# Attention and a gated feed-forward on one core: where transposes and projections stand among the score tiles

## The chip, the core and the metric

The kernel runs on one core of a Trainium2 chip. The metric is the time of one execution on the device in microseconds (us), as the median of several runs. A core has five engines that work side by side and wait for each other through semaphores: TensorE (PE in the profile; its loading of weights is the row PEld), VectorE (DVE), ScalarE (ACT), GpSimd (POOL) and SyncE (SP), which here only starts transfers. Every engine takes its instructions in the order of the program.

## The reference, cut to what matters

Sixteen heads of width 8 over 32 sequences of 256 tokens with 128 features; the distance of two tokens is subtracted from their score. Then a feed-forward of four layers in two halves, and a normalisation after each part.

```python
scores = jnp.einsum('bhid,bhjd->bhij', Q, K) / jnp.sqrt(jnp.float32(hd))
scores = jnp.where(causal_mask, -jnp.inf, scores) + decay
attn = jax.nn.softmax(scores, axis=-1)
out = jnp.einsum('bhij,bhjd->bhid', attn, V) ... @ Wo.T + bo
x = _layernorm(x + out)
h = jax.nn.silu(_tlin(x, w1_w, w1_s)) * _tlin(x, w2_w, w2_s)
h = jax.nn.gelu(_tlin(h, h1_w, h1_s), approximate=False)
h = jax.nn.gelu(_tlin(h, h2_w, h2_s), approximate=False)
x = _layernorm(x + _tlin(h, w3_w, w3_s))
```

## The kernel before

Two sequences make a pair, and there are 16 pairs. `step(n)` (L725) works on several pairs at once: it finishes the attention of pair n, finds the row maxima of pair n+1, projects the queries and keys of pair n+2, ends the feed-forward of pair n-2 and does that of pair n-1. Its first half is a loop of 12 turns (L733), numbered i = 0 to 11 here; its second half is the feed-forward `feed(n - 1)` (L793) with what is left of the attention (`rest`, L761) between its products. The steps from n = 2 to n = 13 are alike; n = 0, 1, 14 and 15 lack some parts.

What a turn of the loop holds, for these steps:

- `weigh(n, i)` (L430): one tile of transposed scores on PE, which the profile calls `s<-qs,ks`, then the exponential on ACT (`e`) and the causal selection on POOL. Every third tile (i = 2, 5, 8, 11) takes the blocks that stand wholly on the diagonal and is called `s_0d` to `s_3d`.
- `row_maxima(n+1, i)` (L373): the same scores the other way round, `s<-ks,qs`, four small products that add the mask (`s<-tri_q,ident_b`), and a maximum on DVE (`m<-s`).
- in some turns a filler on PE. `project(n+2)` (L314, the generator `ahead`) has three: four transposes of x (`pxT`, copied by DVE as `xT`), the queries (`pq`, read by ACT as `qhi` and by DVE as `qlo`) and the keys (`pk`). `last(n-2)` (L648, the generator `settling`) has two: the last layer (`pw3` in the code, shown as `pw<-heven`, which ACT turns into `yT`) and four transposes (`py`, which DVE adds to x1 as `y`). `turn(n-1)` (L538) transposes x1 (`px1T`). `outputs(n, a)` (L470, the generator `side`) has the head outputs `pa` of three score tiles, in two portions, and for every second a the copy `oT` on ACT, four transposes `pt` and the division on DVE (`rec`, `on`).
- at i = 3 DVE also writes the four pieces of `z` for the pair before (`late`, L738).

Two pools in PSUM bind the engines to each other. All score tiles share three buffers of two banks (`ps_s`, L283, tag `s`): a tile can be filled when the one three places earlier has been read, which for `s<-ks,qs` is the exponential of the turn before, and for `s<-qs,ks` the maximum of two turns before. All else shares two buffers of one bank (`ps_w`, L284, tag `work`): `pa` keeps one of them from i = 3 to the copy `oT` at i = 7, and in that time `py`, `pq` and `pk` follow each other through the other one.

The order of all this is written out by hand in the loop, and nothing reorders it (`InOrder`, L50).

PE's products use its array in four ways, which the profile's rows show as rows*columns of the weights: the whole array (128*128: transposes, projections, feed-forward), two halves by rows (64*128 or 62*128: scores), quarters (64*64: the mask), and four strips of columns (128*32: head outputs).

Of the kernel before, what the change touches and what calls it, by code (L numbers as in the profile page):

```python
# [33 lines left out]
G, C = 4, 4  # L34
# [27 lines left out]
def tile_attn_ffn(  # L62
# [96 lines left out]
    def prepare(func):  # L159

        act.activation(nothing, half[:, 0:1], func)
# [124 lines left out]
    def work(nm):  # L286
        return ps_w.tile([P, 512], F32, name=nm, tag="work")

    def two(nm):
        return ps_s.tile([P, 2, 512], F32, name=nm, tag="s")  # L290
# [82 lines left out]
    def row_maxima(n, i):  # L373

        q, k, m = (pairs[n][w] for w in "qkm")
        mv = m.rearrange("i b c (e p g) -> i e p g b c", e=2, p=2)[:, i // 6]
        a, part = divmod(i, 3)
        if part < 2:
            g = 2 * a + part
            s = two(f"s1_{n}_{g}").rearrange("i p (b j) -> i p b j", b=2)  # L380
            for b in range(2):
                for p in range(2):
                    rows = slice(64 * p, 64 * p + ROWS1)
                    pe.matmul(
                        s[:, p, b, :], lhsT=q[rows, g, b * T + P : (b + 1) * T],
                        rhs=k[rows, g, b * T : (b + 1) * T], start=(b == 0), stop=False,
                    )
            mask(lambda p: (s[:, p], P, 2))
            vec.tensor_reduce(mv[:, :, g % C, :, 1], s, AX.X, ALU.max, negate=True)
            return  # L390
        s = two(f"s1_{n}_{a}d").rearrange("i p (h b j) -> i p h b j", h=2, b=2)
        for h in range(2):
            for b in range(2):
                for p in range(2):
                    rows = slice(64 * p, 64 * p + ROWS1)
                    i0 = b * T
                    pe.matmul(
                        s[:, p, h, b, :], lhsT=q[rows, 2 * a + h, i0 : i0 + P],
                        rhs=k[rows, 2 * a + h, i0 : i0 + P],
                        start=(h == 0 and b == 0), stop=False,  # L400
                    )
        mask(lambda p: (s[:, p].rearrange("i h b j -> i (h b) j"), 0, 4))
        vec.tensor_reduce(
            mv[:, :, 2 * a % C : 2 * a % C + 2, :, 0], s, AX.X, ALU.max, negate=True
        )

    def maxima_to_rows(n, halves=(0, 1)):

        q, m = pairs[n]["q"], pairs[n]["m"]
        pm = work(f"pm_{n}_{halves[0]}")  # L410
        e0, rows = halves[0], W * len(halves)
        for t in range(NT):
            pe.transpose(
                pm[0:rows, t * P : (t + 1) * P],
                m[:, t // 2, t % 2, W * e0 : W * e0 + rows], ident,
            )
        hi = mp.tile([H, TOK], F32R, name=f"mhi_{n}_{e0}", tag="mhi", bufs=1)
        act.copy(hi[0:rows, :], pm[0:rows, :])
        lo = mp.tile([H, TOK], F32R, name=f"mlo_{n}_{e0}", tag="mlo", bufs=1)
        vec.tensor_tensor(  # L420
            lo[0:rows, :], pm[0:rows, :], hi[0:rows, :].bitcast(F32), ALU.subtract
        )
        for i, e in enumerate(halves):
            for r, part in enumerate((hi, lo)):
                sp.dma_start(
                    out=q[ROWS1 + r :: 64, C * e : C * e + C, :].bitcast(F32),
                    in_=part[W * i : W * i + W, :].bitcast(F32),
                )
# [41 lines left out]
    def outputs(n, a):  # L470
        v = pairs[n]["v"]
        *first, second = pairs[n][("e", a)]
        r, e = divmod(a, 2)
        if e == 0:
            pairs[n]["pa"] = work(f"pa_{n}_{r}").rearrange("c (b i) -> c b i", b=2)
        pa = pairs[n]["pa"]
        for jc in range(2):
            for b in range(2):
                for c in range(C):
                    h, p = c // 2, c % 2  # L480
                    at = VSLOT * (C * r + c) + VHEAD * e
                    pe.matmul(
                        pa[32 * c : 32 * (c + 1), b, jc * P :],
                        lhsT=v[:, 2 * b + jc, at : at + 32],
                        rhs=second[:, p, h, b, :] if jc else first[h][:, p, b, :],
                        start=(e == b == jc == 0), stop=(e == b == jc == 1),
                        tile_position=(0, 32 * c),
                    )
            if jc == 0:
                yield  # L490
        if e == 0:
            return
        oT = op.tile([P, TOK], F32, name=f"oT_{n}_{r}", tag="oT", bufs=1)
        act.copy(oT, pa.rearrange("c b i -> c (b i)"))
        yield

        if r == 0:
            pairs[n]["on"] = op.tile([P, NT, D], F32, name=f"on_{n}", tag="on", bufs=1)
        on = pairs[n]["on"].rearrange("i t (r e c d) -> i t r e c d", r=2, e=2, c=C)
        po = work(f"pt_{n}_{r}").rearrange("i (t c k) -> i t c k", t=NT, c=C)  # L500
        for t in range(NT):
            pe.transpose(po[:, t].rearrange("i c k -> i (c k)"), oT[:, t * P : (t + 1) * P], ident)
        yield
        rec = mp.tile([P, NT, C, 2], F32, name=f"rec_{n}_{r}", tag="rec")
        vec.reciprocal(rec, po[:, :, :, HD : HD + VHEAD + 1 : VHEAD])
        for e in range(2):
            vec.tensor_tensor(
                on[:, :, r, e], po[:, :, :, VHEAD * e : VHEAD * e + HD],
                rec[:, :, :, e : e + 1].to_broadcast([P, NT, C, HD]), ALU.mult,
            )  # L510
# [19 lines left out]
    def first_norm(n):  # L530
        x1 = x1s[n % 3]
        yield from layernorm(pairs[n]["xb"], x1, f"a_{n}")
        pairs[n] = dict(x1=x1)
# [145 lines left out]
    def run(gen):  # L679
        for _ in gen:  # L680
            pass


    ahead = project(0)
# [7 lines left out]
    ahead = project(1)  # L692
# [32 lines left out]
    def step(n, exact=None, ws=None, hp=None, gp=None):  # L725


        side = iter(())
        settling = (
            last(n - 2, exact, ws, gp) if n > 1 else first_norm(0) if n else inexact_weights()  # L730
        )
        ahead = project(n + 2) if n + 2 < NPAIR else iter(())
        for i in range(3 * G):  # L733
            weigh(n, i)
            j = i + {0: LEAD, 1: -LAG}.get(n, 0)
            if n + 1 < NPAIR and 0 <= j < 3 * G:
                row_maxima(n + 1, j)
            if i == 3 and late:  # L738
                run(late.pop())
            next(side, None)  # L740
            if n and i == 9:
                turn(n - 1, exact)
            if i in ((0, 2) if n > 1 else (0, 2, 4, 6)) if n else i < 11:
                next(settling, None)

            if i in ((3, 4, 5) if n == 1 else (1, 3, 5)):
                next(ahead, None)
            if i % 3 == 2:
                run(side)
                side = outputs(n, i // 3)  # L750
            if n == 0 and i == 3 * G - LEAD:
                maxima_to_rows(1)
        if n < 2:
            run(settling)
        run(ahead)
        if n + 2 < NPAIR:
            stack(n + 2, "q")
            stack(n + 2, "k", sp if n else act)


        def rest():  # L761
            for _ in range(3):
                next(side)
                yield
            if n == 1:
                for i in range(3 * G - LAG, 3 * G):
                    row_maxima(2, i)
                    yield
            if 0 < n < NPAIR - 1:
                maxima_to_rows(n + 1)  # L770
            run(side)
            yield
            if n + 2 < NPAIR:
                project_values(n + 2)
                yield
            last_steps = finish(n)
            next(last_steps)
            yield
            yield from last_steps
            if n:  # L780
                yield
                yield from first_norm(n)
            if n == NPAIR - 1:
                yield
                turn(n, exact)
            if n > 1:
                next(settling)
                late.append(settling)

        if n:  # L790
            prepare(AF.Silu)
        due = rest()
        for _ in feed(n - 1, exact, ws, hp, gp) if n else ():  # L793
            next(due, None)
        run(due)
# [85 lines left out]
```

## Time and profile before

| | us |
|---|---|
| median of 3 runs | 823.32 (823.05 to 824.74) |
| the profiled execution | 824.06 |
| its span, first to last instruction | 822.2 |
| PE busy | 784.6 (95%) |
| DVE busy | 636.0 (77%) |
| ACT busy | 527.5 (64%) |
| POOL busy | 260.8 (32%) |

In the span's 12 alike steps a loop of 12 turns takes 23.27 us (318.45 to 341.72 of the span, the step n = 6), with PE busy for all of it, DVE for 19.90 us and ACT for 16.48 us; the second half of that step takes 24.1 us more. The granted clock of PE is 1.00 there.

How to read the rows: a row of the timeline gives the start in the span, the length, the engine, the line, the operation, out<-in, the shape and how many in a row are merged. Matmuls overlap each other, so the length of a row is longer than the time until the next one starts; what a group of products costs PE is the distance from its start to the start of the next group. In brackets stands the idle time ahead of an instruction and who ended it.

### The profile page before, as it was taken

Reading aid. Unit: us, or ns where it says so; the run is one execution under the profiler, and the core shown is the slowest. Engines: PE = TensorE matmul, PEld = TensorE weight load, DVE = VectorE, ACT = ScalarE, POOL = GpSimd, SP = SyncE. Lnnn points to the kernel's source line nnn. Section 1 sums busy time; section 2 is a strip of 40 time slices with the busy share of each in tenths; the row PEclk is TensorE's granted clock in tenths of the full one; section 3 lists DMA queues with packets and bytes.
Section 4 is the critical chain, followed back from the end, with each engine's and each line's share of the span. In section 5 each row is a group of like instructions: output and inputs, shape, how many; then the busy total and the mean of one; then the engine's idle time right before and its main releaser. Section 6 shows DMA issues by size and latency. Waiting matters only on the chain.

```text
span 822.2 us, 17431 instructions
## 1 busy us (share of the span) xinstructions
PE 784.6 (95%) x7046; PEld 555.8 (68%) x7046; DVE 636.0 (77%) x1247; ACT 527.5 (64%) x719; POOL 260.8 (32%) x341
## 2 busy tenths in 40 slices
PE   4896999999999999999999999999999999999994
PEld 2664676776767677676767767676767767666673
DVE  6786778877887887778788877888878787873674
ACT  5065556766666766766576676667666666758572
POOL 5033413333142333414232342424243231424211
PEclk9879999999999999999999999999999999999998
DMA  6824140403204140410404040130404022000001
GB/s 147 213 62 106 29 92 14 106 15 74 60 14 106 28 107 14 92 42 21 110 17 106 27 101 20 43 90 15 107 26 104 4 62 59 14 4 14 1 8 37
DMA packets 39898, 47.49 MB, mean 58 GB/s; under 512 B 3968, under 2 KB 21632, under 8 KB 39808
## 3 DMA queue, kind: packets, MB, share of 16 engines
q1 hardware_dynamic: 37152, 42.82, 22.0%
q10 hardware_dynamic: 2656, 3.48, 1.9%
q8 instruction: 57, 0.93, 0.5%
q14 instruction: 33, 0.27, 0.1%
HBM read 7.48 MB, written 4.19 MB: 14 GB/s over the span
## 4 chain that ended last, share of the span: by engine, by line
PE 83%; DVE 4%; ACT 3%; issue 1%; DMA 0%; POOL 0%; ACTq 0%; POOLq 0%; DVEq 0%
PE peven L58 14%; PE podd L58 14%; PE s L58 12%; PE pa L58 11%; PE pw L58 10%; PE s_2d L58 2%; PE s_3d L58 2%; PE po L58 2%; PE s_0d L58 2%; PE s_1d L58 2%; PE pt L58 2%; PE pv L58 2%; PE pk L58 2%; PE pq L58 2%; PE px1T L58 1%; PE py L58 1%
## 5 line engine op out<-in xcount | busy, mean ns | idle before, releaser
L58 DVE TENSOR_REDUCE m<-s 128x4 f32<-128x1024 f32 x128 | 155.5, 1218 | 14.6 <-PE s L58 13.3
L58 ACT ACTIVATE e<-s 128x1024 f32<-128x1024 f32 x128 | 130.7, 1022 | 44.2 <-PE s L58 34.2
L463 POOL TENSOR_SCALAR_AFFINE_SELECT e<-e 128x512 f32<-128x512 f32 x128 | 82.6, 646 | 218.5 <-ACT e L58 189.3
L58 PE MATMUL podd<-h,h_near 128*128 128x512 f32 x512 | 131.3, 403 | 1.0 <-DVE m L58 0.5
L58 PE MATMUL peven<-hodd,h_near 128*128 128x512 f32 x512 | 122.7, 396 | 0.0
L58 PEld LDWEIGHTS peven<-hodd,h_near 128*128 128x128 f32 x512 | 95.7, 187 | 23.4 <-DVE hodd L58 0.3
L58 PEld LDWEIGHTS podd<-h,h_near 128*128 128x128 f32 x512 | 91.8, 188 | 23.1 <-DVE h L58 3.2
L58 ACT ACTIVATE hodd<-podd,sh 128x512 fp32r<-128x512 f32 x64 | 44.0, 688 | 62.7 <-PE podd L58 62.6
L58 PE MATMUL pw<-x1T,w_near 128*128 128x512 f32 x256 | 75.6, 418 | 1.1 <-DVE h0w L58 1.1
L274 POOL TENSOR_TENSOR rsa<-rsa,half 128x4 f32<-128x4 f32 x16 | 16.3, 1018 | 176.7 <-DVE rsa L58 176.7
L58 DVE SCALAR_TENSOR_TENSOR h0w<-pw,s,sg 128x512 f32<-128x512 f32 x64 | 47.9, 748 | 30.4 <-ACT sg L58 30.4
L58 PEld LDWEIGHTS s<-qs,ks 64*128 64x128 f32 x512 | 38.9, 188 | 47.7 <-issue 34.1
L58 PE MATMUL pa<-e,vaug 128*32 128x256 f32 x1024 | 70.6, 389 | 0.0
L58 PE MATMUL s<-qs,ks 64*128 64x256 f32 x512 | 65.3, 335 | 0.6 <-ACT e L58 0.5
L58 DVE TENSOR_TENSOR heven<-evenw,heven 128x512 fp32r<-128x512 f32 x64 | 44.2, 692 | 26.6 <-ACT evenw L58 26.1
L58 ACT ACT_TABLE_LOAD x47 | 60.3, 1283 | 3.4 <-issue 2.6
L58 ACT ACTIVATE sg<-pw,s 128x512 f32<-128x512 f32 x64 | 43.7, 684 | 28.2 <-PE pw L58 27.9
L58 PE MATMUL s<-ks,qs 62*128 62x256 f32 x512 | 56.9, 302 | 2.4 <-ACT e_0d L58 1.8
L58 ACT ACTIVATE heven<-peven,sh 128x512 fp32r<-128x512 f32 x48 | 33.4, 696 | 39.8 <-PE peven L58 39.8
L58 PEld LDWEIGHTS pw<-x1T,w_near 128*128 128x128 f32 x256 | 43.4, 188 | 18.4 <-ACT nothing L58 5.8
L581 POOL TENSOR_TENSOR h<-h0w,h 128x512 fp32r<-128x512 f32 x31 | 40.0, 1291 | 43.5 <-DVE h L58 41.2
L58 DVE TENSOR_TENSOR hodd<-oddw,hodd 128x512 fp32r<-128x512 f32 x64 | 43.7, 684 | 10.0 <-ACT oddw L58 9.9
(147 smaller groups left out, 1418.1 us busy)
## 6 DMA issues: line engine op xcount, KB each, us to landing
qs<-qhi SPq DMA_DIRECT2D x32, 256.0 KB
qs<-qlo SPq DMA_DIRECT2D x32, 256.0 KB
ks<-khi SPq DMA_DIRECT2D x26, 256.0 KB
ks<-klo SPq DMA_DIRECT2D x26, 256.0 KB
x<-in_x_dram SPq DMA_DIRECT2D x16, 256.0 KB
out_dram<-z SPq DMA_DIRECT2D x15, 256.0 KB
ks<-khi ACTq DMA_DIRECT2D x6, 256.0 KB
ks<-klo ACTq DMA_DIRECT2D x6, 256.0 KB
```

Of the source, the lines that this page charges most:

```text
L58: return lambda *args, **kw: self.tc.keep_in_program_order(call(*args, **kw))
L274: nc.gpsimd.tensor_tensor(rs, rs, half[:, 0:NT], ALU.pow)
L463: nc.gpsimd.affine_select(out=on_diagonal, in_=on_diagonal, pattern=[[0, on_diagonal.shape[1]], [1, P]], base=0, channel_multiplier=-1, co ...
L581: (nc.gpsimd if o < (1 if final else 2) else vec).tensor_tensor(h[:, 1, o, :], whole, h[:, 0, o, :].bitcast(F32), ALU.subtract)
```

## The change

The loop's fillers stand in other places. `pxT`, the queries and the keys are taken at i = 0, 4 and 6 in place of 1, 3 and 5 (for n = 1 at 3, 4 and 6 in place of 3, 4 and 5). The transposes `py` are taken at i = 3 in place of 2. At i = 9 the transposes `px1T` stand ahead of the head outputs and not behind them. The transposes `pt`, which ran in a turn of their own at i = 8, are kept in `turned` and run at i = 10. The head outputs `pa` stay in turns 3, 4, 6, 7, 9 and 10, now behind the other filler of their turn. So turns 1, 2, 5 and 8 hold score tiles alone, where before every turn but the last had a filler. DVE takes `z` and then `y` between the maxima of turns 3 and 4, where `y` came ahead of the maximum of turn 3 before. No instruction is added or removed, and shapes are the same.

```diff
             if i == 3 and late:
                 run(late.pop())
-            next(side, None)
-            if n and i == 9:
-                turn(n - 1, exact)
-            if i in ((0, 2) if n > 1 else (0, 2, 4, 6)) if n else i < 11:
-                next(settling, None)
-            if i in ((3, 4, 5) if n == 1 else (1, 3, 5)):
-                next(ahead, None)
-            if i % 3 == 2:
-                run(side)
-                side = outputs(n, i // 3)
+            if i in ((3, 4, 6) if n == 1 else (0, 4, 6)):
+                next(ahead, None)
+            if i in ((0, 3) if n > 1 else (0, 2)) if n else i < 11:
+                next(settling, None)
+            if n and i == 9:
+                turn(n - 1, exact)
+            if i == 10:
+                run(turned)
+            if i and i % 3 == 0:
+                turned, side = side, outputs(n, i // 3 - 1)
+            if i % 3 < 2:
+                next(side, None)
             if n == 0 and i == 3 * G - LEAD:
                 maxima_to_rows(1)
+        side = outputs(n, G - 1)
```

## The prediction

> **What bounds the kernel now.** First the page: the busy shares and the chain that ended last.
>
> ```profile
> PE 784.6 (95%) x7046; PEld 555.8 (68%) x7046; DVE 636.0 (77%) x1247; ACT 527.5 (64%) x719; POOL 260.8 (32%) x341
> PE 83%; DVE 4%; ACT 3%; issue 1%; DMA 0%; POOL 0%; ACTq 0%; POOLq 0%; DVEq 0%
> ```
>
> PE is busy nearly always and is 83% of the chain, so a change of order can only help by shortening PE's own groups, and hurts wherever PE starts to wait. So next the timeline of PE, in one of the alike steps (n = 6, loop from 318.45 to 341.72), and the distances between starts.
>
> ```profile
> 305.71 0.60 PE L58 MATMUL pon<-ident,on 128*128 128x128 f32 x4
> 306.07 2.11 PE L58 MATMUL podd<-h,h_near 128*128 128x512 f32 x8
> ...
> 319.31 2.13 PE L58 MATMUL pw<-heven,w_near 128*128 128x512 f32 x8
> 321.37 0.50 PE L58 MATMUL s<-qs,ks 64*128 64x256 f32 x4
> 321.73 0.50 PE L58 MATMUL s<-ks,qs 62*128 62x256 f32 x4
> 322.17 0.25 PE L58 MATMUL s<-tri_q,ident_b 64*64 64x128 bf16 x4
> 322.35 0.66 PE L58 MATMUL pxT<-ident,x 128*128 128x128 f32 x4
> 322.93 0.66 PE L58 MATMUL s_0d<-qs,ks 64*128 64x128 f32 x8
> ```
>
> Four transposes cost 0.36 us ahead of a product on the whole array (305.71 to 306.07) and 0.58 ahead of a score tile (322.35 to 322.93): leaving one way of using the array costs about 0.22. That is what the change can save. What it can lose shows in step n = 14, which has no `pxT`, `pq` or `pk`, so that its turn 1 is already bare:
>
> ```profile
> 701.33 0.25 PE L58 MATMUL s<-tri_q,ident_b 64*64 64x128 bf16 x4
> 701.51 0.66 PE L58 MATMUL s_0d<-qs,ks 64*128 64x128 f32 x8
> 702.39 0.66 PE L58 MATMUL s_0d<-ks,qs 62*128 62x128 f32 x8 [0.21 <-ACT e L58]
> 702.98 0.30 PE L58 MATMUL s_0d<-tri_q,ident_b 64*64 64x256 bf16 x4
> 703.22 0.66 PE L58 MATMUL py<-ident,yT 128*128 128x128 f32 x4
> ```
>
> Mask to score costs 0.18 (701.33 to 701.51), as mask to `pxT` does (322.17 to 322.35), so bare turns have no junction price. But the second tile waits for the exponential whose buffer it takes: 0.88 from 701.51 where 0.50 is usual (322.93 to 323.43), and 0.59 in place of 0.54 behind it, 0.43 in all.
>
> **The change, part by part**, in us. I write a usual turn from the timeline of n = 6: first tile 0.34, second 0.34, mask 0.18, so 0.86; with the diagonal tile (turns 2, 5, 8, 11) 0.50, 0.54, 0.24, so 1.28.
>
> *Saved: one merged junction.* `pxT` now stands directly ahead of the last layer, both on the whole array. 0.22 goes; I take 0.20, since `pon` above had itself come from the whole array. In n = 6 the second tile of turn 1 also waits a little for the first exponential: 321.37 to 322.17 is 0.80 against 0.68 usual. `pxT` ahead of it makes that tile 0.41 later, and 0.12 goes too.
>
> *Not saved: the other five junctions.* `py`, `pq`, `pk`, `px1T` and `pt` now stand ahead of head outputs and those ahead of scores. From the second half of step n = 6:
>
> ```profile
> 341.72 1.19 PE L58 MATMUL pw<-x1T,w_near 128*128 128x512 f32 x4
> 342.85 1.07 PE L58 MATMUL pa<-e,vaug 128*32 128x256 f32 x16
> ...
> 345.55 1.18 PE L58 MATMUL pw<-x1T,w_near 128*128 128x512 f32 x4
> 346.57 0.60 PE L58 MATMUL pt<-ident,oT 128*128 128x128 f32 x4
> ```
>
> Whole array to head outputs is 1.13, to whole array 1.02: leaving it is not free. The trace has no transposes or f32 projection ahead of `pa`. The junction may cost anything from 0 (a gain of 0.22 each) to the 0.22 of now; I take 0.22, because the 1.13 row loses 0.11 and the last layer ahead of scores about the same (2.06 against 1.98, 306.07 to 308.05, for eight products). Head outputs cost 1.00 ahead of `pq` and of scores alike. The Trainium skill (TensorEngine Tiling (Array Packing), Key Properties) says that changing the tiling mode drains the engine; counted by that rule alone a loop goes from 25 changes to 24, so by it the change saves one drain, which agrees with the rows (0.58 against 0.36 at the one junction that goes). The same page (Performance Considerations, PSUM Bottleneck) warns that faster tiles leave the emptying of PSUM as the limit, which speaks against bare turns; the 0.21 of idle in turn 1 of n = 14 agrees.
>
> *Added: waits.* Now I walk a step from its first tile (0.00) in the new order, with 0.05 to 0.07 from an engine's end to the start of who waits (the mask ends at 322.17 + 0.25 = 322.42, its maximum on DVE starts at 322.49). ACT first:
>
> ```profile
> 320.67 1.01 ACT L58 ACTIVATE e<-s 128x1024 f32<-128x1024 f32 x1
> 321.58 0.68 ACT L58 ACTIVATE yT<-pw,s 128x512 f32<-128x512 f32 x1
> 322.15 1.03 ACT L58 ACTIVATE e<-s 128x1024 f32<-128x1024 f32 x1
> ```
>
> Turn 0: tiles and mask to 0.86, `pxT` to 1.27, last layer to 3.30. ACT's `yT` can begin when the last layer ends, 1.27 + 2.13 + 0.05 = 3.45, the exponential of turn 1 follows 0.57 later at 4.02 (321.58 to 322.15) and ends at 5.05. Turn 1 is bare: tiles at 3.30 and 3.64, mask 3.98, and the first tile of turn 2 at 4.16. The second tile of turn 2 takes the buffer of that exponential: it could start at 4.66 and starts at 5.10. **Wait 0.44, with the 0.05 behind it 0.49**, as n = 14 shows.
>
> Turn 2 then has its mask at 5.69. Turn 3: 5.93 to 6.79, `py` to 7.37, `pa` to 8.37; turn 4: to 9.23, and there stands `pq`. It needs a `work` buffer. `pa` holds one, so `pq` takes that of `py`, free only when DVE has read it as `y`. The DVE of now:
>
> ```profile
> 325.50 0.68 DVE L58 TENSOR_TENSOR y<-py,x 128x512 f32<-128x512 f32 x1
> 326.09 1.21 DVE L58 TENSOR_REDUCE m<-s 128x4 f32<-128x1024 f32 x1
> 327.23 1.11 DVE L58 TENSOR_SCALAR z<-y,mvf,rsf 128x128 f32<-128x128 f32 x4
> 328.54 0.75 DVE L58 SCALAR_TENSOR_TENSOR qlo<-pq,bq_sb,qhi 128x512 fp32r<-128x512 f32 x1 [0.21 <-ACT qhi L58]
> ```
>
> Now `y` is done at 326.18 and `pq` starts at 326.65: covered by 0.47. In the new order DVE takes the maximum of turn 2, that of turn 3, `z`, then `y`. The maximum of turn 2 starts when its mask ends, 5.69 + 0.30 + 0.07 = 6.06; the next 1.14 later (326.09 to 327.23), `z` again 1.14 later at 8.34, `y` 1.03 later at 9.37, done at 10.05, `pq` at 10.10 in place of 9.23. **Wait 0.87.** Behind `pq` on PE everything waits: PE is in order. In step n = 2 there is no `z`, and this wait is gone.
>
> Turns 5 and 8 are bare and diagonal. The second tile of turn 6 waits for the exponential of turn 5: 0.66 for the tile, 0.05, 1.02, 0.05, so 1.78 from its start, while PE is there after 1.28 + 0.34 = 1.62: 0.16, and a scores tile that had to wait costs about 0.10 more behind it (321.73 to 322.17 is 0.44 in place of 0.34). **0.26, and 0.26 again at turn 9.** In n = 14 turn 5 is bare already, and mask 708.12 to `pa` 709.53 is 1.41 where 0.24 + 0.86 = 1.10 is usual: 0.31, which bears out the size. `pt` needs the buffer of `px1T`, free after its copies on ACT and DVE: by the same walk some 0.3 ahead of it.
>
> The loop's other PE work, ACT's table loads, DMAs and the feed-forward are unchanged; SP's transfers of queries and keys need the step's last scores anyway, and are issued behind them as before. A later `pk` (turn 6 for 5) has at least 15 us until they go out.
>
> *Sum.* A step: -0.20 - 0.12 + 0.49 + 0.87 + 0.26 + 0.26 = **+1.56**. PE is busy from end to end of the second half, so nothing is given back there. Twelve alike steps: 18.7, less 0.87 for n = 2: 17.9. Step 14 gets the wait of turn 9: 0.3. For n = 1 two bare turns cost 0.3 to 0.5, and the wait of `pk` for `qlo` (0.29 of idle at 89.62) goes: 0. In n = 0 DVE has a maximum and a comparison of weights (1.22 + 0.69) in most turns, more than PE; in n = 15 the exponentials and selections lead: 0, within 1 both ways. In all +18.2. The profiled execution took 824.06, so 842.3; it stood 0.74 above the median of 823.32, so **841.5**.
>
> **Rivals.**
> 1. *`pq` does not wait.* If it gets a free buffer, or DVE is not that late, 1.56 - 0.87 = 0.69 a step, 8.6 in all: 832. Against it: two buffers and `pa` in one of them.
> 2. *The junction ahead of head outputs is free, and the change is faster.* Place: the five fillers ahead of `pa`. Price: up to 0.22 x 5 = 1.1 a step. With the full wait of `pq` that leaves +0.46 a step, 829; with that wait covered too, 0.69 - 1.1 = -0.41, some -5: 818. It is faster from a junction under 0.22 - 0.69/5 = 0.08, and only if `pq` is free. For it: 0.36 against 0.58; against it: the 1.13 row.
> 3. *Waits pile up.* DVE is busy 19.9 of 23.27 us of the loop already. If `qlo`, `klo` and the maxima fall behind after `y`, `pk` and `pt` wait too, 0.5 to 1 a step: 848 to 853.
> 4. *Idle is only moved*, and nothing is measured: 823. PE's solid busy row speaks against it.
>
> **How the numbers follow.** Forecast (836 to 848) 0.74; rival 1 0.08; rival 2 0.08, of it 0.06 on the fast side and 0.02 at 829; rival 3 0.06; rival 4 0.04. A measurement of this kernel can tell 0.2% (1.6 us) from no change. Slower: 0.74 + 0.08 + 0.02 + 0.06 = 0.90; same 0.04; faster 0.06. The range 831 to 850 takes in the forecast, rival 1 and the low end of rival 3; it leaves out rivals 2 and 4 and the rest of 3, some 0.15.
>
> **What would show it.** PE's `pq` with about 0.9 of idle ended by DVE `y` in steps 3 to 13 and not in 2; `s_0d<-ks,qs` waiting 0.2 to 0.4 for ACT `e`; the second tiles of turns 6 and 9 waiting for `e_1d` and `e_2d`; a loop of 24.8 us in place of 23.27; `py`, `px1T`, `pt` to `pa` at 0.58, and `pxT` to the last layer at 0.41. Wrong would be 0.36 to 0.4 for the transposes ahead of `pa`, or `pq` starting right behind its mask.

## The result, and the profile after

The changed kernel takes 847.11 us as the median of four runs (846.53 to 847.73) against 823.45 us for the kernel before (823.32 in the table above, which has one run less): a ratio of 1.0282, with a 95% interval of 1.0266 to 1.0298. It is slower by 2.8%. The forecast was 841.5 us, in a range from 831 to 850. The profiled execution has a span of 845.7 us, 23.5 more than before.

The page first, the busy shares and the chain:

```profile
PE 792.5 (94%) x7046; PEld 557.7 (66%) x7046; DVE 636.3 (75%) x1247; ACT 530.9 (63%) x719; POOL 258.7 (31%) x341
...
PE 72%; ACT 12%; DVE 10%; DMA 3%; issue 2%; POOL 0%; SPq 0%; ACTq 0%; POOLq 0%; DVEq 0%
```

The instructions are the same in number and nearly so in busy time, but PE's part of the chain falls from 83% to 72%, and ACT and DVE, 3% and 4% before, are 12% and 10%: PE now waits for them. Where it waits is in the timeline of PE, here turns 0 to 6 of step n = 6 (loop from 327.48 to 352.41):

```profile
328.33 0.66 PE L58 MATMUL pxT<-ident,x 128*128 128x128 f32 x4
328.74 2.11 PE L58 MATMUL pw<-heven,w_near 128*128 128x512 f32 x8
...
331.64 0.66 PE L58 MATMUL s_0d<-qs,ks 64*128 64x128 f32 x8
332.55 0.66 PE L58 MATMUL s_0d<-ks,qs 62*128 62x128 f32 x8 [0.25 <-ACT e L58]
333.14 0.30 PE L58 MATMUL s_0d<-tri_q,ident_b 64*64 64x256 bf16 x4
...
334.23 0.66 PE L58 MATMUL py<-ident,yT 128*128 128x128 f32 x4
334.81 1.07 PE L58 MATMUL pa<-e,vaug 128*32 128x256 f32 x16
...
336.49 0.25 PE L58 MATMUL s<-tri_q,ident_b 64*64 64x128 bf16 x4
337.53 1.13 PE L58 MATMUL pq<-xT,wq_sb 128*128 128x512 f32 x2 [0.79 <-DVE y L58]
338.58 0.65 PE L58 MATMUL pa<-e_0d,vaug 128*32 128x128 f32 x16
...
340.43 0.50 PE L58 MATMUL s<-qs,ks 64*128 64x256 f32 x4
341.00 0.50 PE L58 MATMUL s<-ks,qs 62*128 62x256 f32 x4
341.43 0.25 PE L58 MATMUL s<-tri_q,ident_b 64*64 64x128 bf16 x4
```

Read as distances between starts: `pxT` to the last layer is 0.41, as the merged junction should be. The second tile of turn 2 starts 0.91 behind the first in place of 0.50. `pq` starts 1.04 behind its mask in place of 0.18, and the bracket names DVE's `y`. The second tile of turn 6 starts 0.57 behind the first and the mask 0.43 behind that, some 0.33 more together than in a usual turn. Turn 9 has the same (346.36 to 346.93 to 347.36). No bracket names who ended this wait; it is read from ACT, whose exponential of turn 5, in the buffer that this tile takes, ends at 339.92 + 1.02 = 340.94, just ahead of 341.00:

```profile
339.92 1.02 ACT L58 ACTIVATE e_1d<-s_1d 128x1024 f32<-128x1024 f32 x1 [0.54 <-PE s_1d L58]
```

But `py` to `pa` is 0.58 and `pq` to `pa` 1.05, what they cost ahead of score tiles before.

DVE at the same place, with `y` now behind the maximum of turn 3 and behind `z`:

```profile
333.50 1.23 DVE L58 TENSOR_REDUCE m<-s_0d 128x8 f32<-128x1024 f32 x1 [0.48 <-PE s_0d L58]
334.64 1.22 DVE L58 TENSOR_REDUCE m<-s 128x4 f32<-128x1024 f32 x1
335.77 1.11 DVE L58 TENSOR_SCALAR z<-y,mvf,rsf 128x128 f32<-128x128 f32 x4
336.79 0.68 DVE L58 TENSOR_TENSOR y<-py,x 128x512 f32<-128x512 f32 x1
```

DVE works from 333.50 without a gap and ends `y` at 336.79 + 0.68 = 337.47; `pq` starts at 337.53. A loop of an alike step takes 24.93 to 24.97 us in place of 23.27; that of step 2, which has no `z`, takes 24.06, and that of step 13 takes 25.23, 0.3 more, because the second tile of its turn 9 starts 0.86 behind the first. The second halves stay at 24.1 us (24.4 in step 11).

### The profile page after: what moved, and what is told of

It reads as the page before. It is cut to its first block, busy times and chain, and to the rows that moved or that the text cites. A ratio compares the mean times of both kernels' runs of the same rounds, so it can differ in the third digit from the quotient of the medians.

```text
span 845.7 us, 17408 instructions
## 1 busy us (share of the span) xinstructions
PE 792.5 (94%) x7046; PEld 557.7 (66%) x7046; DVE 636.3 (75%) x1247; ACT 530.9 (63%) x719; POOL 258.7 (31%) x341
## 4 chain that ended last, share of the span: by engine, by line
PE 72%; ACT 12%; DVE 10%; DMA 3%; issue 2%; POOL 0%; SPq 0%; ACTq 0%; POOLq 0%; DVEq 0%
PE peven L58 14%; PE podd L58 14%; PE pw L58 10%; PE pa L58 9%; PE s L58 7%; DVE m L58 4%; ACT e L58 4%; PE s_3d L58 2%; PE po L58 2%; ACT e_2d L58 2%; PE pq L58 2%; ACT e_1d L58 2%; PE pt L58 2%; PE s_0d L58 2%; PE pk L58 2%
## 5 line engine op out<-in xcount | busy, mean ns | idle before, releaser
L58 PE MATMUL pa<-e,vaug 128*32 128x256 f32 x1024 | 72.3, 397 | 0.5 <-POOL e L463 0.5
L58 PE MATMUL s<-ks,qs 62*128 62x256 f32 x512 | 59.5, 312 | 4.3 <-ACT e L58 2.3
```

Source lines behind the costliest of these rows:

```text
L58: return lambda *args, **kw: self.tc.keep_in_program_order(call(*args, **kw))
```

## The experiments

Times are medians. Each group shares runs of the kernel before on its chip, which took 823.6 to 824.0 us there. In brackets stands the ratio to these, with its 95% interval.

**`z` behind `y`.** In the changed kernel the block with `late` goes behind the last layer's step:

```diff
-            if i == 3 and late:
-                run(late.pop())
...
                 next(settling, None)
+            if i == 3 and late:
+                run(late.pop())
```

> The changed kernel, with the four pieces of z put behind the sum y in turn 3. Theory (pq waits for y because py holds its PSUM buffer): y ends 1.03 us earlier, which covers the wait of pq (the mask to pq distance is 1.05 us in the changed kernel where 0.18 is usual), so 0.87 us goes in each of 11 steps: 9.5 us less than the changed kernel's 847.1, about 837.6. Rival (pq waits for its own input or another buffer, or DVE is late as a whole): no change, 847, or the wait moves to another product behind it.

Measured: 838.0 us (1.0178, 1.0163 to 1.0194), 9.1 less than the changed kernel. PE and then DVE in a step's turns 3 and 4:

```profile
331.78 0.66 PE L58 MATMUL py<-ident,yT 128*128 128x128 f32 x4
...
334.04 0.25 PE L58 MATMUL s<-tri_q,ident_b 64*64 64x128 bf16 x4
334.22 1.12 PE L58 MATMUL pq<-xT,wq_sb 128*128 128x512 f32 x2
```

```profile
332.19 1.22 DVE L58 TENSOR_REDUCE m<-s 128x4 f32<-128x1024 f32 x1
333.32 0.68 DVE L58 TENSOR_TENSOR y<-py,x 128x512 f32<-128x512 f32 x1
333.92 1.11 DVE L58 TENSOR_SCALAR z<-y,mvf,rsf 128x128 f32<-128x128 f32 x4
```

`y` ends at 334.00, before PE gets to `pq`, which follows its mask by 0.18 again. Nothing on PE was moved; the loops from step 3 on are 24.07 to 24.09 us (24.36 in step 13), 0.87 shorter. So the wait of `pq` is one for the buffer of `py`, and its price is the forecast's 0.87.

**The bare turns 5 and 8 filled again.** In the changed kernel, for n > 1:

```diff
-            if i in ((3, 4, 6) if n == 1 else (0, 4, 6)):
+            if i in ((3, 4, 6) if n == 1 else (0, 4, 6 if n == 0 else 5)):
...
-            if i == 10:
-                run(turned)
+            if i == (10 if n < 2 else 8):
+                run(turned if n < 2 else side)
```

> The changed kernel, with the keys pk back in turn 5 and the transposes pt back in turn 8 for n > 1, so that only turns 1, 2 and 11 are bare; pk and pt then stand ahead of score tiles again. Theory (bare turns make the next turn's second score tile wait for an exponential, and the junction costs the same ahead of head outputs and of scores): 0.33 us less at each of turns 6 and 9, twice in 12 to 14 steps: 8 to 9 us less, about 839; if pk has to wait for qlo, 2 to 3 us of that comes back. Rival (leaving the whole array is cheaper ahead of head outputs): the two junctions cost up to 0.22 us each again, and the gain shrinks to 3 us.

Measured: 843.3 us (1.0241, 1.0226 to 1.0257), 3.8 less, not 8 to 9. The size agrees with the rival, and the rival is wrong all the same, as PE shows in turns 5, 6, 8 and 9:

```profile
338.97 1.13 PE L58 MATMUL pk<-xT,wk_sb 128*128 128x512 f32 x2
340.02 0.51 PE L58 MATMUL s<-qs,ks 64*128 64x256 f32 x4
340.36 0.40 PE L58 MATMUL s<-ks,qs 62*128 62x256 f32 x4
340.70 0.25 PE L58 MATMUL s<-tri_q,ident_b 64*64 64x128 bf16 x4
...
344.58 0.66 PE L58 MATMUL pt<-ident,oT 128*128 128x128 f32 x4
345.16 0.50 PE L58 MATMUL s<-qs,ks 64*128 64x256 f32 x4
...
346.01 0.66 PE L58 MATMUL px1T<-ident,x 128*128 128x128 f32 x4
346.93 1.07 PE L58 MATMUL pa<-e,vaug 128*32 128x256 f32 x16 [0.26 <-DVE on L58]
```

`pk` costs 1.05 and `pt` 0.58 ahead of the score tiles, what they cost ahead of head outputs in the changed kernel, so no junction grew dearer. Turn 6 is usual again (0.34, 0.34), and so is turn 9: the 0.66 of the bare turns went. But `px1T` to `pa` is 0.92 in place of 0.58. `pt` in turn 8 and `px1T` in turn 9 now hold the two `work` buffers when the next `pa` wants one, and it waits until DVE has read `pt` (`on` ends at 346.79). The loop falls from 24.95 to 24.56: 0.66 gained, some 0.3 turned into a new wait of the same kind as that of `pq`. The expectation had placed such a wait at `pk`, which did not wait.

**The merged junction alone.** In the kernel before, `pxT` alone goes from turn 1 to turn 0, ahead of the last layer, for n > 1:

```diff
+            if n > 1 and i == 0:
+                next(ahead, None)
             if i in ((0, 2) if n > 1 else (0, 2, 4, 6)) if n else i < 11:
                 next(settling, None)
...
-            if i in ((3, 4, 5) if n == 1 else (1, 3, 5)):
+            if i in ((3, 4, 5) if n == 1 else (3, 5) if n else (1, 3, 5)):
```

> The kernel before, with pxT alone moved, from turn 1 to directly ahead of the last layer in turn 0 (n > 1); all else stays, so turn 1 alone is bare. Theory: a loop of an alike step gains 0.20 for the junction and 0.12 for the wait that turn 1 has now, and loses 0.43 to 0.49 to the bare turn: 0.1 to 0.2 us longer, 23.4 us, 1 to 2 us in all, 825. Rival (the merged junction is the gain and the bare turn costs nothing by itself): 0.32 less in each of 12 steps, 820.

Measured: 825.5 us (1.0019, 1.0011 to 1.0028), slower by a hair. The loop takes 23.41 us, 0.14 more. Its timeline has the merged junction at 0.41 and the wait of turn 2:

```profile
319.87 0.66 PE L58 MATMUL pxT<-ident,x 128*128 128x128 f32 x4
320.28 2.11 PE L58 MATMUL pw<-heven,w_near 128*128 128x512 f32 x8
...
323.17 0.66 PE L58 MATMUL s_0d<-qs,ks 64*128 64x128 f32 x8
324.08 0.66 PE L58 MATMUL s_0d<-ks,qs 62*128 62x128 f32 x8 [0.25 <-ACT e L58]
```

A junction saved and a turn left bare for it: the turn costs more.

**The start.** The first tile of step 2 comes at 128.92 us before and at 132.02 after, which the forecast did not have. Step 0 alone was tried first, then the steps 0 and 1 with their old loop, then step 1 with its old loop and `pt` of step 0 in turn 8; the kernels with an old loop in a step keep the old lines for that n and the new ones else. The edit for `pt`:

```diff
-            if i == 10:
-                run(turned)
+            if i == (10 if n else 8):
+                run(turned if n else side)
```

> The changed kernel, with the transposes pt of step n = 0 alone put back into turn 8. Theory: the start lost 3.1 us because in turn 10 pt takes one of the two work buffers, DVE reads it only behind the comparisons of weights, and the transposed maxima pm wait for that buffer (2.16 us of idle ended by DVE on). With pt two turns earlier pm waits as before: about 3 us less, 844. Rival (the start is late because of the bare turns of n = 0, or the lower clock there): no change within 0.5 us.

> The changed kernel with the loop of steps n = 0 and n = 1 as in the kernel before; n > 1 is as changed. Theory: the first tile of step 2, at 132.0 us in the changed kernel, comes at 128.8 to 130.1 again, where the kernels with the old start have it: 2 to 3 us less than 847.1, 844 to 845. Rival (the start came late by the granted clock alone): 847, and the first tile of step 2 near 132.

> The changed kernel with pt of step n = 0 alone in turn 8, a second time, on the same chip as the kernel with the whole old start. Theory (the wait of pm for the buffer of pt is the greater part of the late start): at least 1.5 us less than the changed kernel, 845 to 845.5, and within 1 us of the kernel with the old start. Rival (what pm gains is lost again in step 1): 846 to 847, as the first time.

> The changed kernel with pt of step 0 in turn 8 and the whole loop of step n = 1 as in the kernel before. Of the 3.0 us that the old start gave back (844.1 for 847.1), pt in turn 8 alone gave back 0.9 to 1.2. Theory (the rest lies in the new order of step 1): 844 to 844.5, as with the whole old start. Rival (the rest lies in the other moves of step 0): 845.5 to 846, as with pt alone.

> The changed kernel itself, once more, beside the kernel above on the same chip, so that differences under 1 us can be read: 846.5 to 847.7 by the runs so far. If it comes under 846.3, the split of the start's 3 us is not to be read from runs on different chips.

| kernel | median | first tile of step 2, in its profile |
|---|---|---|
| changed | 847.11 | 132.02 |
| changed, again | 848.66 | 133.43 |
| `pt` of step 0 in turn 8 | 846.17 | 131.85 |
| the same, again | 845.91 | 131.71 |
| that, and step 1 as before | 844.89 | 129.90 |
| steps 0 and 1 as before | 844.09 | 128.39 |

By these medians the start costs 3.0 to 4.6 us. The changed kernel came out 1.5 us longer the second time, outside the 846.5 to 847.7 that was expected, so medians of different groups split the start no finer than that. In step 0 of the changed kernel PE's timeline has three long waits:

```profile
57.73 0.66 PE L58 MATMUL s_2d<-ks,qs 62*128 62x128 f32 x8 [0.28 <-ACT e_1d L58]
...
64.22 0.66 PE L58 MATMUL s_3d<-ks,qs 62*128 62x128 f32 x8 [0.61 <-ACT e_2d L58]
...
66.48 0.66 PE L58 MATMUL pt<-ident,oT 128*128 128x128 f32 x4
67.07 0.64 PE L58 MATMUL pa<-e_2d,vaug 128*32 128x128 f32 x16
69.87 0.60 PE L58 MATMUL pm<-ident,m 128*16 128x128 f32 x4 [2.16 <-DVE on L58]
```

and the last of these rows in the kernel before, then with `pt` in turn 8 (second run):

```profile
66.75 0.60 PE L58 MATMUL pm<-ident,m 128*16 128x128 f32 x4 [0.77 <-DVE m L58]
```

```profile
68.18 0.60 PE L58 MATMUL pm<-ident,m 128*16 128x128 f32 x4 [0.72 <-DVE m L58]
```

`pm`, the transposed maxima of pair 1, takes a `work` buffer too, and `pt` in the same turn holds one until DVE, late with the comparisons of weights, has made `on`. `pm` starts at 69.87 in place of 66.75, and from there to step 2 both kernels take 62.2 us, so the whole 3.1 has come about by then. The wait of `pm` is 1.4 of it, from the head outputs to `pm` 2.80 in place of 1.42. The second tiles behind the bare turns 5 and 8 wait for exponentials, which makes 0.5 each from the turn's first tile to its mask (56.95 to 58.32 where it was 57.37 to 58.20, and 63.10 to 64.81 where it was 62.50 to 63.67). Another 0.55 is in turn 4, whose score tiles now stand ahead of `pq` and take 1.41 in place of 0.86; the granted clock from 50 to 55 us is 0.57, and 0.72 before. So the rival of the first trial, bare turns and the clock, has a little more than half, though no run changes these two alone.

With `pt` in turn 8, which then is not bare either, `pm` waits for its maxima alone and starts 1.5 and 1.7 us sooner. Yet step 2 starts only 0.2 and 0.3 sooner, and the median fell by 0.9 and 1.2: less than either theory asked for (3 us, and at least 1.5), while the rival of the second trial had it, that what `pm` gains is lost again behind it. Step 1 as before gives about 1 more, between its theory and its rival. In step 1 the changed kernel's bare turns cost 0.33 twice (92.04 to 92.61 to 93.04, and 97.98 to 98.55 to 98.98). What takes the gain away behind `pm` is not settled: there the granted clock is not the same from profile to profile (78 to 91 us: 1.00 with the whole old start, 0.87 in the changed kernel and 0.50 in its second profile, 0.74 with `pt` in turn 8), and the old start itself puts step 2 at 128.4 to 130.1 us in the profiles of the kernels that have it.

**Versions meant to beat both.** For n > 1, the kernel before with these lines in its loop:

```diff
+                if i in (0, 1, 5):
+                    next(ahead, None)
+                if i in (0, 2):
+                    next(settling, None)
+                if i == 9:
+                    turn(n - 1, exact)
+                for _ in range({9: 0, 10: 2}.get(i, 1)):
+                    next(side, None)
```

> A version meant to beat both: the kernel before for n = 0 and 1; for n > 1 pxT directly ahead of the last layer in turn 0, pq in turn 1, py in turn 2, head outputs in 3, 4, 6 and 7, pk in turn 5, pt in turn 8, px1T in turn 9, and both portions of the third head outputs together in turn 10. No turn but the last is bare, and a step has two junctions less. Theory: 0.20 for the merged pxT, 0.12 for the wait of turn 1, 0.11 for the joined head outputs, 0.43 us in each of 12 steps: 5 us less than before, about 818. Rival (any other order runs into waits, or the idle only moves): 823 or more.

Measured: 819.09 us (0.9942, 0.9929 to 0.9956), faster than the kernel before. PE in turns 0 to 2 and 10 of step n = 6:

```profile
318.70 0.66 PE L58 MATMUL pxT<-ident,x 128*128 128x128 f32 x4
319.12 2.11 PE L58 MATMUL pw<-heven,w_near 128*128 128x512 f32 x8
321.16 0.50 PE L58 MATMUL s<-qs,ks 64*128 64x256 f32 x4
321.49 0.41 PE L58 MATMUL s<-ks,qs 62*128 62x256 f32 x4
321.83 0.25 PE L58 MATMUL s<-tri_q,ident_b 64*64 64x128 bf16 x4
322.01 1.12 PE L58 MATMUL pq<-xT,wq_sb 128*128 128x512 f32 x2
323.07 0.66 PE L58 MATMUL s_0d<-qs,ks 64*128 64x128 f32 x8
323.56 0.61 PE L58 MATMUL s_0d<-ks,qs 62*128 62x128 f32 x8
...
337.96 1.07 PE L58 MATMUL pa<-e,vaug 128*32 128x256 f32 x16
338.85 0.62 PE L58 MATMUL pa<-e_2d,vaug 128*32 128x128 f32 x16
339.40 0.66 PE L58 MATMUL s_3d<-qs,ks 64*128 64x128 f32 x8
```

The same merged junction, but turn 1 has `pq` and the second tile of turn 2 does not wait (0.49 behind the first). The joined head outputs take 0.89 + 0.55 = 1.44 where they took 1.00 + 0.57. The loop is 22.82 us, 0.45 shorter.

The second version also joins the two portions of the last head outputs, in the second half (`rest`):

```diff
-            for _ in range(3):
-                next(side)
-                yield
+            next(side)
+            next(side)
+            yield
+            yield
+            next(side)
+            yield
```

> The version with joined head outputs (819.1), and in the feed-forward both portions of the last head outputs together behind the first product as well, where they stood behind the first and the second. Theory: one visit to head outputs less in 15 second halves; leaving the whole array, entering the strips and coming back cost 0.1 each way by the rows 1.13 against 1.02, so 0.2 us in each of 15: 3 us less, about 816. Rival (the last diagonal selection on POOL is not done, or the score buffers of the first layer run out): no gain, 819 or more.

Measured: 820.98 us (0.9968, 0.9957 to 0.998); no gain on the version above. The loops stay at 22.8, and the second halves go from 24.1 to 24.36 (that of step 14 from 25.06 to 26.87). Loading of weights ahead of the first products of the next layer:

```profile
349.59 0.30 PEld L58 LDWEIGHTS podd<-h,h_near 128*128 128x128 f32 x2 [0.43 <-DVE h L58]
350.31 0.30 PEld L58 LDWEIGHTS podd<-h,h_near 128*128 128x128 f32 x2 [0.43 <-DVE h L58]
```

The head outputs between the first layer's products had given ACT and DVE time to make `h`. The first sixteen products of the next layer take 4.34 us now (346.56 to 350.90) where the kernel before has 3.80 (300.94 to 304.74).

## Why the prediction was right, and where a size was off

- *Merged junction, 0.20, and the wait of turn 1, 0.12:* right, the first a little less. `pxT` to the last layer is 0.41 in 12 steps, as the walk had it, but from 0.58 that is a gain of 0.17; turn 1 is a usual 0.85 (330.79 to 331.64), a gain of 0.13.
- *Turn 2's wait, 0.49:* 0.91 and 0.59 measured, so 0.46. The walk gave the last layer 2.03 (1.27 to 3.30) where its own row has 2.06; with 2.06 it comes to 0.46 too.
- *`pq`, 0.87, in steps 3 to 13 and not in 2:* right, shown by moving `z`. Rival 1 falls.
- *The other junctions cost what they did:* right. `py` and `px1T` to `pa` 0.58, `pt` 0.59, `pq` and `pk` 1.05. Rival 2 falls.
- *Turns 6 and 9, 0.26 each:* mis-sized, 0.33 each. The tile itself waits 0.23 and not 0.16; the 0.10 behind it is right. The row of n = 14 in the forecast, 0.31, was the better one to take.
- *A step, +1.56:* measured +1.68 in the steps with `z` but 13, which has +1.96, and +0.80 in step 2 (forecast +0.69). DVE caught up behind `y`, so rival 3 falls, and nothing was given back in the second half, so rival 4 falls.
- *The sum, +17.9 for twelve steps:* 19.6 in the profiles.
- *"n = 1: 0" and "n = 0 and n = 15: 0, within 1 both ways":* this is the term that was most off. The first tile of step 2 is 3.1 us later, the loop of n = 15 0.59 longer (there `pt` has 1.03 of idle ended by DVE's `x1T`, which reads the buffer of `px1T`); that of n = 14 is 0.32 longer (forecast 0.3). For n = 0 I argued from DVE being busier than PE and didn't ask who takes the buffer of a moved `pt`, the question that had found the wait of `pq`, nor carry over the waits behind bare turns, which step 0 has as well.

The terms add up: 19.6 + 3.1 + 0.6 + 0.3, and 0.3 more in the second halves less 0.4 behind the last loop, is 23.5, the difference of the spans.

The drain on a change of tiling mode, which the forecast took from the Trainium skill (TensorEngine Tiling (Array Packing), Key Properties), agrees with the rows where a visit is saved: 0.17 for the merged transposes, 0.13 for joined head outputs. That it is a drain that costs this, no run here shows by itself. Counted with the quarters as a way of their own, a loop goes from 38 changes to 37 and not from 25 to 24; the difference of one stands. What follows the product made no difference.

## What to carry to other kernels

In a loop like this one, whose score tiles share three buffers, a filler between two tiles is not only a junction to be paid for: it is the time in which other engines empty the buffer that the next tile wants, and a turn left bare gives that time away, so merge junctions only as long as each turn keeps one filler. When an instruction is moved, ask for every buffer that it takes who held it last, on which engine that reader stands, and what has come to stand ahead of it there: here this one question decides `pq`, `pm` and the `pa` that waited for `pt`.

## What the runs showed of the hardware

A score tile that had to wait starts its successor late as well: 0.43 from the waiting second tile to its mask in place of 0.33, in the turns shown, even where the wait was a few hundredths (before, turn 1: 321.73 to 322.17). The cost of leaving the whole array didn't depend on what came next, strips of columns or halves by rows: 0.58 both ways for four transposes, 1.05 for a projection.
